# Attention with 64-wide heads: outputs moved ahead of undivided transposes, separate PSUM banks for scores, reciprocal sums through DRAM and scaled on GpSimd

## The chip, the core and the metric

The kernel runs on one core of a Trainium2 chip. The metric is the time of one launch in microseconds of the device. The engines are named as the profile names them: PE (TensorE), with its weight loads listed apart as PEld; DVE (VectorE), ACT (ScalarE), POOL (GpSimd), and SP (SyncE), which here only issues DMAs.

## What is computed

The program is four residual layers on x of shape 4 x 1024 x 256, float32: linear attention, a mixture of experts, causal softmax attention, and a second block with rotary attention and experts. The change touches the third layer alone. With a layernorm of x as its input (called x below) it computes

```python
q = (x @ Wq).reshape(B, S, 16, 64)
k = (x @ Wk).reshape(B, S, 16, 64)
v = (x @ Wv).reshape(B, S, 16, 64)
scores = einsum('bqhd,bkhd->bhqk', q / sqrt(64), k) + causal_mask
attn = softmax(scores, axis=-1)
out = einsum('bhqk,bkhd->bqhd', attn, v).reshape(B, S, 1024)
return x + out @ Wo
```

and the caller adds the layernorm of that to its residual. B is 4, S is 1024.

## The kernel before

The class `CausalAttention` (lines 670 to 923) works through 32 pairs: four batches, and in each eight pairs of heads, so that two heads of 64 fill the 128 rows of a tile. Each pair has eight steps, one for each block i of 128 query rows. The order of instructions on PE, DVE and ACT is written out by hand (`manual_schedule` in `run`, line 700); the order on POOL and SP is made by the scheduler.

For one step (b, hp, i) there are these parts:

- `scores` (L798): for one or two chunks of up to 512 keys, two matmuls, one for each head (L810), the heads in different halves of the array's rows. Blocks 0 to 3 have one chunk, blocks 4 to 7 have two. On DVE, a plain maximum over a full first chunk (L824), and for the last chunk a custom operation that adds the causal mask, negates, and takes the minimum (L819). With two chunks, L830 takes the smaller of both minima. Then ACT makes the exponentials with this bias and sums them as it goes (L839).
- At blocks 3 and 7 the end of `scores` turns the sums of four blocks into reciprocals on DVE (L850 to L853), and GpSimd spreads them over 64 columns for each head (L855).
- `turn` (L858): the exponentials are transposed in blocks of 128 (L867), four to a PSUM bank. The banks are copied to SBUF by `Ctx.copy`, which gives copies to DVE (L100) and ACT (L102) by turns. `turn` is called twice a step, with one half of the banks each; the second call also transposes the spread reciprocals at blocks 3 and 7 (L875) and copies them by ACT into rT (L879).
- `values` (L881): outputs as v times the transposed exponentials (L891), the two heads in different halves of the array's columns, into the bank ps_o, which holds four blocks. After blocks 3 and 7, DVE multiplies ps_o by rT into oT (L902).

Beside them, at blocks 2, 3 and 4, `project` makes q, k (L788) and v (L775) of the next pair, one for each block. In the first pair of batches 1 to 3, `finish` multiplies the previous batch's oT by Wo (L909), and `add` puts its layernorm onto x. The layernorms' powers run on POOL (L116), as do these additions (L921); the sums are stored by SP (kept, L923). In the last pairs of a batch, `measure`, `norm` and `flip` prepare the next batch's input.

The order within a step is that of the loop in `run`: scores of the next step, first half of `turn` for this step, the preparations and projections, `values` of the step before, second half of `turn`. On PE, ACT and DVE instructions start in that order.

PSUM has eight banks. Seven of them rotate under one tag, `bank`, for scores, transposes, projections and everything else of this stage (L805); the eighth is ps_o.

Of the kernel before, what the change touches and what calls it, by code (L numbers as in the profile page):

```python
# [9 lines left out]
F32 = mybir.dt.float32  # L10
# [3 lines left out]
ALU = mybir.AluOpType  # L14
# [5 lines left out]
P = 128  # L20
# [4 lines left out]
TPB = L // P  # L25
# [10 lines left out]
H3, HD3 = 16, 64  # L36
# [5 lines left out]
MASK = -(2.0**100)  # L42
# [627 lines left out]
class CausalAttention:  # L670
# [5 lines left out]

    NP = H3 // 2
    G = 4

    def __init__(self, k, pool, Wq, Wk, Wv, Wo):  # L680
        nc = k.nc
        self.k, self.pool = k, pool
        self.wq = per_chunk(nc, pool, Wq, "l1_wq")
        self.wk = per_chunk(nc, pool, Wk, "l1_wk")
        self.wv = per_chunk(nc, pool, Wv, "l1_wv")
        self.wo = pool.tile([P, self.NP, D], F32, name="l1_wo")
        nc.sync.dma_start(self.wo, Wo.rearrange("(c p) n -> p c n", p=P))

        self.wide_mask = pool.tile([P, 512], F32, name="l1_mask")
        nc.vector.memset(self.wide_mask, 0.0)  # L690
        nc.vector.tensor_copy(self.wide_mask[:, 512 - P :], k.mask)
        self.xn, self.xT, self.qk, self.v, self.oT = {}, {}, {}, {}, {}
        self.st, self.added = {}, {}
        self.e, self.eT, self.o, self.sums, self.r = {}, {}, {}, {}, {}

    def run(self, x, kept):

        pairs = [(b, hp) for b in range(B) for hp in range(self.NP)]
        steps = [(b, hp, i) for b, hp in pairs for i in range(TPB)]
        with self.k.tc.manual_schedule(engines=ENGINES):  # L700
            for j in range(TPB):
                self.measure(x, 0, j)
            for j in range(TPB):
                self.norm(x, 0, j)
                self.flip(0, j)
            for w in range(3):
                self.project(0, 0, w)
            self.scores(steps[0])
            for n, step in enumerate(steps):
                b, hp, i = step  # L710
                if n + 1 < len(steps):
                    self.scores(steps[n + 1])
                self.turn(step, 0)
                if b + 1 < B:

                    at = n % (self.NP * TPB) - (self.NP - 3) * TPB
                    if 0 <= at < TPB:
                        self.measure(x, b + 1, at)
                    if 0 <= at - 5 < TPB:
                        self.norm(x, b + 1, at - 5)  # L720
                    if 0 <= at - 7 < TPB:
                        self.flip(b + 1, at - 7)
                after = n // TPB + 1
                if 2 <= i < 5 and after < len(pairs):
                    self.project(*pairs[after], i - 2)
                if b > 0:

                    at = hp * TPB + i - 1
                    if 0 <= at < TPB:
                        self.finish(b - 1, at)  # L730
                    if 0 <= at - 2 < TPB:
                        self.add(x, b - 1, at - 2, kept)
                if n > 0:
                    self.values(steps[n - 1])
                self.turn(step, 1)
            self.values(steps[-1])
            for j in range(TPB + 2):
                if j < TPB:
                    self.finish(B - 1, j)
                if j >= 2:  # L740
                    self.add(x, B - 1, j - 2, kept)
# [56 lines left out]
    def scores(self, step):  # L798
        k, nc, pool = self.k, self.k.nc, self.pool
        b, hp, i = step  # L800
        qT, kT = self.qk[b, hp]
        n = (i + 1) * P
        parts, nms = [], []
        for c in range(0, n, 512):
            w = min(512, n - c)  # L805
            last = c + w == n
            ps = [k.bank("ps_s") for _ in range(2)]
            for a in range(2):
                rows = slice(a * HD3, (a + 1) * HD3)
                nc.tensor.matmul(  # L810
                    ps[a][:, :w], qT[rows, i * P : (i + 1) * P], kT[rows, c : c + w],
                    start=True, stop=True,
                )
            nm = k.small.tile([P, 2], F32, tag="nm3", name="nm", bufs=6)
            for a in range(2):
                s = ps[a][:, :w]
                if last:

                    nc.vector.tensor_tensor_reduce(  # L819
                        out=s, in0=s, in1=self.wide_mask[:, 512 - w :], scale=-1.0,  # L820
                        scalar=-MASK, op0=ALU.add, op1=ALU.min, accum_out=nm[:, a : a + 1],
                    )
                else:
                    nc.vector.tensor_reduce(nm[:, a : a + 1], s, AX.X, ALU.max, negate=True)  # L824
            parts.append((c, w, ps, -1.0 if last else 1.0))
            nms.append(nm)
        nm = nms[0]
        if len(nms) > 1:
            nm = k.small.tile([P, 2], F32, tag="nm3", name="nm", bufs=6)
            nc.vector.tensor_tensor(nm, nms[0], nms[1], ALU.min)  # L830
        if i % self.G == 0:
            self.sums[b, hp, i // self.G] = k.small.tile(
                [P, self.G, 2, i // self.G + 1], F32, tag=f"sums{i // self.G}", name="sums", bufs=2
            )
        sums = self.sums[b, hp, i // self.G]
        es = [pool.tile([P, L], F32, tag="e", name="e", bufs=4)[:, :n] for _ in range(2)]
        for c, w, ps, sign in parts:
            for a in range(2):
                nc.scalar.activation(  # L839
                    es[a][:, c : c + w], ps[a][:, :w], AF.Exp, bias=nm[:, a : a + 1], scale=sign,  # L840
                    accum_out=sums[:, i % self.G, a, c // 512 : c // 512 + 1],
                )
        self.e[step] = [e[:, t * P : (t + 1) * P] for e in es for t in range(i + 1)]
        self.eT[step] = []
        if i % self.G == self.G - 1:

            sums = self.sums.pop((b, hp, i // self.G))
            r = k.small.tile([P, self.G, 2], F32, tag="r3", name="r3", bufs=2)
            if i // self.G:
                nc.vector.tensor_tensor(r, sums[:, :, :, 0], sums[:, :, :, 1], ALU.add)  # L850
                nc.vector.reciprocal(r, r)  # L851
            else:
                nc.vector.reciprocal(r, sums[:, :, :, 0])  # L853
            wide = pool.tile([P, self.G, 2, HD3], F32, tag="rw", name="rw", bufs=1)
            nc.gpsimd.tensor_copy(wide, r.unsqueeze(3).to_broadcast([P, self.G, 2, HD3]))  # L855
            self.r[step] = wide

    def turn(self, step, half):  # L858

        k, nc, pool = self.k, self.k.nc, self.pool  # L860
        blocks = self.e[step]
        banks = [blocks[c : c + 4] for c in range(0, len(blocks), 4)]
        at = len(banks) // 2
        for some in banks[at:] if half else banks[:at]:
            pt = k.bank("ps_eT")
            for j, block in enumerate(some):
                nc.tensor.transpose(pt[:, j * P : (j + 1) * P], block, k.ident)  # L867
            eT = pool.tile([P, 512], F32, tag="eT", name="eT", bufs=8)
            k.copy(eT[:, : len(some) * P], pt[:, : len(some) * P])
            self.eT[step] += [eT[:, j * P : (j + 1) * P] for j in range(len(some))]  # L870
        if half == 1 and step in self.r:
            wide = self.r.pop(step)
            pt = k.bank("ps_r")
            for j in range(self.G):
                nc.tensor.transpose(  # L875
                    pt[:, j * P : (j + 1) * P], wide[:, j].rearrange("p a d -> p (a d)"), k.ident
                )
            self.rT = pool.tile([P, self.G * P], F32, tag="rT", name="rT", bufs=2)
            nc.scalar.copy(self.rT, pt)  # L879

    def values(self, step):  # L881
        k, nc, pool = self.k, self.k.nc, self.pool
        b, hp, i = step
# [4 lines left out]
        at = i % self.G * P  # L888
# [7 lines left out]
        if i % self.G == self.G - 1:  # L896
            part = b, i // self.G
            if hp == 0:
                self.oT[part] = pool.tile(
                    [P, self.NP, self.G * P], F32, tag="oT", name="oT", bufs=2  # L900
                )
            nc.vector.tensor_tensor(self.oT[part][:, hp, :], self.o, self.rT, ALU.mult)  # L902

    def finish(self, b, j):
        k, nc = self.k, self.k.nc
# [872 lines left out]
def sandwich(ctx, tc, w, out):  # L1778
# [23 lines left out]
                    moe.always(b - 1)  # L1802
        moe.run(x)
    with ExitStack() as stage:
        k.open_psum(stage, "psum3", banks=7)
        pool = stage.enter_context(tc.tile_pool(name="attn", bufs=1, reuse_waits="tile"))
        attn = CausalAttention(k, pool, w["Wq1"], w["Wk1"], w["Wv1"], w["Wo1"])
        attn.run(x, kept)
    with tc.tile_pool(name="keep", bufs=1, reuse_waits="tile") as keep:
        with ExitStack() as rope:  # L1810
# [76 lines left out]
```

## Time and profile before

| what | us |
|---|---|
| median of three runs (lowest to highest) | 3917.28 (3915.67 to 3919.04) |
| the profiled execution, its own time | 4002.54 |
| its span, first to last instruction | 4000.8 |
| this stage within the span | 967 to 2405 |
| ps_s L810, PE busy, 1536 records | 349.0 |
| ps_eT L867, PE busy, 2304 records | 351.0 |
| ps_o L891, PE busy, 4608 records | 317.7 |
| ps_r L875, PE busy, 256 records | 38.4 |
| e L839, ACT busy, with its sums | 437.0 |
| oT L902, DVE, 64 of | 0.692 each |
| rw L855, POOL, 64 of | 0.616 each |

A float32 matmul appears as two records, a transpose as one. A profile row gives the engine, the line of the kernel, and what is written and read ("ps_eT<-ident,e"), then, in the timeline, start and duration, and in brackets how long the engine had been idle and what ended that. The end of a matmul is modelled, so what PE really does is better read from the starts of its weight loads (PEld), each of which must wait for the bank or operand that its matmul needs.

### The profile page before, as it was taken

Reading aid. Unit: us, or ns where it says so; the run is one execution under the profiler, and the core shown is the slowest. Engines: PE = TensorE matmul, PEld = TensorE weight load, DVE = VectorE, ACT = ScalarE, POOL = GpSimd, SP = SyncE. Lnnn points to the kernel's source line nnn. Section 1 sums busy time; section 2 is a strip of 40 time slices with the busy share of each in tenths; the row PEclk is TensorE's granted clock in tenths of the full one; section 3 lists DMA queues with packets and bytes.
Section 4 is the critical chain, followed back from the end, with each engine's and each line's share of the span. In section 5 each row is a group of like instructions: output and inputs, shape, how many; then the busy total and the mean of one; then the engine's idle time right before and its main releaser. Section 6 shows DMA issues by size and latency. Waiting matters only on the chain.

```text
span 4000.8 us, 55924 instructions
## 1 busy us (share of the span) xinstructions
PE 3562.7 (89%) x21560; PEld 2224.5 (56%) x21560; DVE 1904.2 (48%) x5757; ACT 1480.0 (37%) x3593; POOL 786.2 (20%) x1088
## 2 busy tenths in 40 slices
PE   5899988867999999999999995999898997799982
PEld 4555666634666766766676673344334443466652
DVE  3645211145556556555655554667667574211124
ACT  1231111113555355445535542456455544011111
POOL 0101566552000100010010003222121111211033
PEclk7798999988999999999999997899899998799996
DMA  2001455521000000000000000000000001433213
GB/s 73 22 22 33 129 155 157 149 72 63 1 1 1 12 1 1 1 12 1 1 9 4 1 4 23 1 6 6 6 4 9 1 8 21 100 85 74 74 53 121
DMA packets 90882, 151.50 MB, mean 38 GB/s; under 512 B 19923, under 2 KB 66966, under 8 KB 90486
## 3 DMA queue, kind: packets, MB, share of 16 engines
q0 software_dynamic: 24816, 77.59, 7.5%
q1 hardware_dynamic: 42710, 47.51, 3.8%
q10 hardware_dynamic: 23088, 22.81, 1.7%
q8 instruction: 170, 2.79, 0.3%
q14 instruction: 98, 0.80, 0.1%
HBM read 112.35 MB, written 35.52 MB: 37 GB/s over the span
## 4 chain that ended last, share of the span: by engine, by line
PE 78%; DVE 9%; issue 4%; ACT 3%; POOL 2%; another core or an unknown queue 2%; DMA 1%; SPq 0%; ACTq 0%; POOLq 0%; DVEq 0%
PE ps_s L810 8%; PE ps_eT L867 7%; PE ps_gu L549 7%; PE ps_o L891 7%; PE ps_main L1253 7%; PE ps_qk L788 6%; PE ps_y L1751 6%; PE ps_h L1741 5%; PE ps_sums L1337 4%; PE ps_y L566 3%; PE ps_v L775 3%; PE ps_wo L909 3%; PE ps_exp L1309 2%; PE ps_main L1418 2%
## 5 line engine op out<-in xcount | busy, mean ns | idle before, releaser
L839 ACT ACTIVATE e<-ps_s,nm 128x512 f32<-128x512 f32 (+3 forms) x768 | 437.0, 578 | 491.1 <-DVE nm L830 332.0
L1316 ACT ACTIVATE et<-ps_exp 128x512 f32<-128x512 f32 (+3 forms) x744 | 325.5, 490 | 299.3 <-PE ps_exp L1309 263.6
L1309 PE MATMUL ps_exp<-qT,kT 32*128 32x512 f32 (+3 forms) x1488 | 408.4, 561 | 5.4 <-ACT et L1316 3.2
L1253 PE MATMUL ps_main<-kT,qT 32*128 32x512 f32 (+3 forms) x1488 | 384.0, 562 | 3.4 <-DVE nm L1266 2.5
L867 PE MATMUL ps_eT<-ident,e 128*128 128x128 f32 x2304 | 351.0, 284 | 6.2 <-ACT e L839 6.2
L810 PE MATMUL ps_s<-kT,qT 64*128 64x512 f32 (+3 forms) x1536 | 349.0, 521 | 1.6 <-ACT e L839 1.1
L891 PE MATMUL ps_o<-eT,v 128*64 128x128 f32 x4608 | 317.7, 279 | 3.3 <-DVE eT L100 3.2
L867 PEld LDWEIGHTS ps_eT<-ident,e 128*128 128x128 f32 x2304 | 243.4, 140 | 138.1 <-issue 62.3
L1266 DVE CUSTOM_DVE_ANT_0 ps_main<-ps_main,wide_mask 128x512 f32<-128x512 f32 (+1 forms) x488 | 230.8, 514 | 171.0 <-PE ps_exp L1309 122.3
L891 PEld LDWEIGHTS ps_o<-eT,v 128*64 128x64 f32 x4608 | 251.1, 136 | 102.0 <-issue 70.0
L819 DVE CUSTOM_DVE_ANT_0 ps_s<-ps_s,l_mask 128x128 f32<-128x128 f32 (+3 forms) x512 | 240.9, 512 | 54.4 <-PE ps_s L810 51.1
L549 PE MATMUL ps_gu<-moe_xTb,moe_w 128*128 128x256 f32 (+1 forms) x936 | 218.9, 384 | 46.9 <-DVE hT L557 31.8
L824 DVE TENSOR_REDUCE nm<-ps_s 128x1 f32<-128x512 f32 x256 | 166.7, 687 | 186.0 <-PE ps_s L810 186.0
L855 POOL COPY rw<-r 128x512 f32<-128x512 f32 x64 | 39.3, 615 | 1080.4 <-DVE r L851 651.9
L557 DVE TENSOR_TENSOR hT<-sg,ps_gu 128x256 f32<-128x256 f32 (+1 forms) x165 | 80.4, 495 | 343.4 <-ACT sg L556 145.8
L1741 PE MATMUL ps_h<-xT,w 128*128 128x512 f32 x512 | 227.4, 603 | 12.9 <-issue 12.9
L1253 PEld LDWEIGHTS ps_main<-kT,qT 32*128 32x128 f32 x1488 | 139.0, 195 | 179.5 <-issue 60.1
L102 ACT COPY eT<-ps_eT 128x512 f32<-128x512 f32 x320 | 169.0, 551 | 174.8 <-PE ps_eT L867 174.8
L1746 ACT ACTIVATE hTe<-ps_h,b 128x1024 f32<-128x1024 f32 x64 | 71.2, 1114 | 433.8 <-PE ps_h L1741 388.8
L1751 PE MATMUL ps_y<-w,hTe 128*128 128x256 f32 x1024 | 225.3, 382 | 4.2 <-ACT hTe L1746 4.2
L100 DVE COPY eT<-ps_eT 128x512 f32<-128x512 f32 (+1 forms) x320 | 197.3, 623 | 53.3 <-PE ps_eT L867 52.0
L1751 PEld LDWEIGHTS ps_y<-w,hTe 128*128 128x128 f32 x1024 | 196.1, 192 | 35.5 <-ACT hTe L1746 5.1
(366 smaller groups left out, 5858.7 us busy)
## 6 DMA issues: line engine op xcount, KB each, us to landing
w<-in_W SPq DMA_DIRECT2D x16, 1024.0 KB
moe_out<-moe_yb ACTq DMA_DIRECT2D x39, 256.0 KB
slots_out<-y ACTq DMA_DIRECT2D x8, 1024.0 KB
x<-in_x SPq DMA_DIRECT2D x4, 1024.0 KB
moe_in<-moe_xn ACTq DMA_DIRECT2D x4, 1024.0 KB
kept<-x SPq DMA_DIRECT2D x16, 256.0 KB
rows_in<-t SPq DMA_DIRECT2D x32, 128.0 KB
xo<-kept SPq DMA_DIRECT2D x8, 512.0 KB
```

The lines of the kernel that those rows point to most:

```text
L549: nc.tensor.matmul(ps[:n, half * 512 : half * 512 + W], w[:, c, f * P : f * P + n], xT[:, c, cols], start=(c == 0), stop=(c == NC - 1),)
L788: nc.tensor.matmul(ps, w[:, c, hp * P : (hp + 1) * P], xT[:, c, h : h + 512], start=(c == 0), stop=(c == NC - 1),)
L810: nc.tensor.matmul(ps[a][:, :w], qT[rows, i * P : (i + 1) * P], kT[rows, c : c + w], start=True, stop=True,)
L819: nc.vector.tensor_tensor_reduce(out=s, in0=s, in1=self.wide_mask[:, 512 - w :], scale=-1.0, scalar=-MASK, op0=ALU.add, op1=ALU.min, accum ...
L839: nc.scalar.activation(es[a][:, c : c + w], ps[a][:, :w], AF.Exp, bias=nm[:, a : a + 1], scale=sign, accum_out=sums[:, i % self.G, a, c // ...
L867: nc.tensor.transpose(pt[:, j * P : (j + 1) * P], block, k.ident)
L891: nc.tensor.matmul(self.o[a * HD3 : (a + 1) * HD3, at : at + P], v[:, t, a, :], eT[a * (i + 1) + t], start=(t == 0), stop=(t == i),)
L1253: self.k.nc.tensor.matmul(ps[:, :w], self.qT[b, h][rows, g, i % 4 * P : (i % 4 + 1) * P], self.kT[b, c // 512][rows, g, :w], start=True, s ...
L1309: self.k.nc.tensor.matmul(ps, self.kT[b, t // 4][rows, g, t % 4 * P : (t % 4 + 1) * P], self.qT[b, h][rows, g, off:], start=True, stop=True,)
L1316: self.k.nc.scalar.activation(et[:, r, 512 - ps.shape[1] :], ps, AF.Exp)
L1741: nc.tensor.matmul(ps[:, h : h + 512], w1[:, c, f * P : (f + 1) * P], xT[:, c, h : h + 512], start=(c == 0), stop=(c == NC - 1),)
L1751: nc.tensor.matmul(ps[:, :D], hT[:, f, s * P : (s + 1) * P], w2[:, f, :], start=(f == 0), stop=(f == nf - 1),)
```

## The change

Five things change together.

- The order of a step becomes: scores of the next step, `values` of the step before, then the whole of `turn` for this step, then preparations, projections and `finish` (which comes one step earlier than it did).
- Scores get four PSUM banks of their own (tag `s`). The other uses share the remaining three; ps_o keeps its bank.
- The plain maximum of the first chunk goes as a starting scalar into the custom operation of the last chunk, so that L830 is gone.
- The spreading on GpSimd and the transposes of reciprocals are gone. Instead SP stores the reciprocals to DRAM, transposed, in two DMAs, and reads them back in two, each broadcast over 64 partitions, into rT.
- ps_o is copied to oT by `Ctx.copy`, and GpSimd multiplies oT by rT in place.

```diff
-    def __init__(self, k, pool, Wq, Wk, Wv, Wo):
+    SB = 4
+    def __init__(self, k, pool, dram, Wq, Wk, Wv, Wo):
...
+        self.r_there = [
+            dram.tile([2, self.G, P], F32, name=f"l1_r{g}") for g in range(TPB // self.G)
+        ]
...
                 if n + 1 < len(steps):
                     self.scores(steps[n + 1])
-                self.turn(step, 0)
+                if n > 0:
+                    self.values(steps[n - 1])
+                self.turn(step)
...
-                    at = hp * TPB + i - 1
+                    at = hp * TPB + i
...
-                if n > 0:
-                    self.values(steps[n - 1])
-                self.turn(step, 1)
...
-            ps = [k.bank("ps_s") for _ in range(2)]
+            ps = [
+                k.psum.tile([P, 512], F32, tag="s", name="ps_s", bufs=self.SB) for _ in range(2)
+            ]
...
+                    least = nms[0][:, a : a + 1] if nms else -MASK
                     nc.vector.tensor_tensor_reduce(
                         out=s, in0=s, in1=self.wide_mask[:, 512 - w :], scale=-1.0,
-                        scalar=-MASK, op0=ALU.add, op1=ALU.min, accum_out=nm[:, a : a + 1],
+                        scalar=least, op0=ALU.add, op1=ALU.min, accum_out=nm[:, a : a + 1],
                     )
...
-        nm = nms[0]
-        if len(nms) > 1:
-            nm = k.small.tile([P, 2], F32, tag="nm3", name="nm", bufs=6)
-            nc.vector.tensor_tensor(nm, nms[0], nms[1], ALU.min)
+        nm = nms[-1]
...
-            wide = pool.tile([P, self.G, 2, HD3], F32, tag="rw", name="rw", bufs=1)
-            nc.gpsimd.tensor_copy(wide, r.unsqueeze(3).to_broadcast([P, self.G, 2, HD3]))
-            self.r[step] = wide
+            self.totals(step)
+
+    def totals(self, step):
...
+        there = self.r_there[g]
+            for a in range(2):
+                nc.sync.dma_start(there[a].rearrange("j q -> q j"), r[:, :, a])
+        rT = self.r[b, hp, g] = self.pool.tile([P, self.G * P], F32, tag="rT", name="rT", bufs=3)
+        for a in range(2):
+            nc.sync.dma_start(
+                rT[a * HD3 : (a + 1) * HD3],
+                there[a].rearrange("j q -> (j q)").partition_broadcast(HD3),
+            )
...
-        banks = [blocks[c : c + 4] for c in range(0, len(blocks), 4)]
-        at = len(banks) // 2
-        for some in banks[at:] if half else banks[:at]:
+        for c in range(0, len(blocks), 4):
+            some = blocks[c : c + 4]
...
-        if half == 1 and step in self.r:
-            wide = self.r.pop(step)
-            pt = k.bank("ps_r")
-            for j in range(self.G):
-                nc.tensor.transpose(
-                    pt[:, j * P : (j + 1) * P], wide[:, j].rearrange("p a d -> p (a d)"), k.ident
-                )
-            self.rT = pool.tile([P, self.G * P], F32, tag="rT", name="rT", bufs=2)
-            nc.scalar.copy(self.rT, pt)
...
-            nc.vector.tensor_tensor(self.oT[part][:, hp, :], self.o, self.rT, ALU.mult)
+            oT = self.oT[part][:, hp, :]
+            k.copy(oT, self.o)
+            nc.gpsimd.tensor_tensor(oT, oT, self.r.pop((b, hp, i // self.G)), ALU.mult)
...
-        k.open_psum(stage, "psum3", banks=7)
+        k.open_psum(stage, "psum3", banks=7 - CausalAttention.SB)
```

## The prediction

> **What bounds the kernel now.** I looked first at the stage that the change touches, 967 to 2405 us of the span, and at one head pair inside it, in the busy times by window (columns: window, length, then busy us and instructions of PE, PEld, DVE, ACT, POOL, then clock, DMA share, GB/s):
> ```profile
> 967.00:2405.00 1438.00, 1426.85 (x10752) 968.22 (x10752) 805.97 (x2242) 702.19 (x2027) 93.04 (x148) 1.00 0.01 4
> 1151.05:1192.61 41.56, 41.38 (x321) 27.39 (x321) 25.56 (x74) 21.82 (x64) 3.41 (x6) 1.00 0.01 1
> ```
> PE looks busy for 99% of it, at full clock, beside half-busy DVE and ACT. [...] PEld is 66%. By busy time, nothing but PE work counts, and the change would save the 38.4 us busy of the ps_r transposes: 3917 - 38 = 3879. By weight loads, PE has room for waits, and these decide. I go by the second.
>
> So I read PE from one weight load to the next. The timeline of a middle pair, first the step that starts with scores of block 5, then the one of block 7:
> ```profile
> 1151.05 0.30 PEld L810 LDWEIGHTS ps_s<-kT,qT 64*128 64x128 f32 x4 [0.17 <-issue]
> ...
> 1152.21 1.29 DVE L824 TENSOR_REDUCE nm<-ps_s 128x1 f32<-128x512 f32 x2 [2.19 <-PE ps_s L810]
> ...
> 1153.42 0.42 DVE L819 CUSTOM_DVE_ANT_0 ps_s<-ps_s,l_mask 128x256 f32<-128x256 f32 x1
> 1153.76 0.14 DVE L819 DVE_READ_ACCUMULATOR2_ANT nm<- 128x1 f32 x1
> ...
> 1154.31 0.16 DVE L830 TENSOR_TENSOR nm<-nm 128x2 f32<-128x2 f32 x1
> ...
> 1154.57 0.69 ACT L839 ACTIVATE e<-ps_s,nm 128x512 f32<-128x512 f32 x1 [2.77 <-DVE nm L830]
> ...
> 1156.36 0.48 ACT L839 ACTIVATE e<-ps_s,nm 128x256 f32<-128x256 f32 x1
> ...
> 1156.81 0.59 ACT L102 COPY v<-ps_v 128x512 f32<-128x512 f32 x1
> ```
> ```profile
> 1163.15 0.29 PEld L810 LDWEIGHTS ps_s<-kT,qT 64*128 64x128 f32 x2 [0.23 <-ACT e L839]
> ...
> 1164.94 0.29 PEld L810 LDWEIGHTS ps_s<-kT,qT 64*128 64x128 f32 x2 [0.27 <-ACT e L839]
> ...
> 1167.27 0.69 ACT L839 ACTIVATE e<-ps_s,nm 128x512 f32<-128x512 f32 x1 [1.42 <-DVE nm L830]
> ...
> 1169.94 0.87 ACT L102 COPY eT<-ps_eT 128x512 f32<-128x512 f32 x2
> ...
> 1170.16 0.17 DVE L850 TENSOR_TENSOR r<-sums 128x8 f32<-128x8 f32 x1 [2.99 <-ACT e L839]
> ```
> ACT takes nothing else until a step's exponentials are done: 5.8 us after S(5) began, 6.8 after S(7). After S(7) DVE waits for them too. Copies of transposes queue behind. PE survives this now because seven banks rotate. The waits by pair of waiter and releaser give the same picture (us in total, times, longest):
> ```profile
> ACT e L839 <- DVE nm L830: 332.0, 128, 3.6
> ...
> DVE r L850 <- ACT e L839: 94.6, 32, 3.0
> ...
> PEld ps_s L810 <- ACT e L839: 34.9, 123, 0.5
> ```
>
> **The yardstick.** S(i), O(i), T(i) are the scores, outputs and all transposes of block i; a prime marks the next pair. Scores' first weight loads stand at 1151.05, 1158.53, 1163.15, 1169.28, 1174.69, 1177.59, 1179.44, 1185.48 and 1192.61, so the steps that begin with S(5), S(6), S(7), S(0'), S(1'), S(2'), S(3'), S(4') take 7.48, 4.62, 6.13, 5.41, 2.90, 1.85, 6.04 and 7.13: 41.56 a pair.
>
> Slots on PE, also from the weight loads: a transpose 0.107; an output record 0.053; a 512-wide score pair 0.85, narrower in proportion; q or k 3.63; v 3.77; and 0.17 to 0.20 at each change between scores, outputs and full-tile work.
>
> **Part by part.** (1) *ps_r goes.* Four transposes are 0.43, twice a pair: -0.85. ACT loses its 0.59 copy, off the path. (2) *Outputs move ahead of undivided transposes.* Scores-half-outputs-half becomes scores-outputs-transposes: one tile change less in seven steps of eight, 7 x 0.17 = -1.19. (3) *The minimum (L830) goes.* Exponentials of head 0 can start after its own mask row: 1153.76 + 0.14 + 0.04 = 2.89 after S(5), not 3.52; S(7) likewise 3.18 instead of 4.12. Whether the mask operation takes longer with a scalar from memory no row shows: between 0 and about 0.4 us (both heads' rows then come before ACT starts); I take 0, as L121, which reads two such scalars for 256 elements, takes 0.41 like the plain 256 copy, 0.42.
>
> (4) *Three banks for everything but scores and ps_o.* I took the order of the built changed program, which names the instruction each one waits for, and laid the durations above along it, from each step's start:
>
> S(5): S 1.49, O(3) 1.02, T(4) from 2.51 to 3.58 in three banks. v needs T(4)'s first bank, which ACT copies after the exponentials: 2.89 + 0.67 + 0.67 + 0.45 + 0.45 = 5.13, copy to 5.72, 0.14 for the release: 5.86. A wait of **2.28**. v 3.77: step **9.63**.
> S(6): 1.71 + O(4) 1.24 + T(5) 1.45 = **4.40**, no wait.
> S(7): its second pair needs the bank of S(6)'s last exponential, free at 5.63 of the step before: **0.35**, O(5) at 2.25, T(6) at 3.71. T(6)'s fourth bank is its first, copied by ACT after 3.18 + 4 x 0.67 = 5.86, free at 6.59 where PE came at 4.99: **1.60**. Step **6.97**. DVE, held by the reciprocal to 6.4, copies the second bank by 7.08, soon enough.
> S(0'): 0.41 + O(6) 1.66 + T(7) 1.88 with **0.14** for the fourth bank: **4.09**.
> S(1'): **2.90** and S(2'): **1.85**, as before; ps_o is copied by ACT at 3.31, needed at 3.79.
> S(3'): O(1') needs T(1')'s copy, behind the exponentials of S(2'): **0.59**. With O(1'), T(2') and q: **6.51**.
> S(4'): 1.28 + 0.81 + 0.85 + k 3.63 = **6.57**.
>
> Sum 42.92, of which 4.96 is new waits. Without these PE needs 37.96; today's 41.56 is that plus 0.85, 1.19 and 1.55 of waits which go. So 3.60 gained, 4.96 lost: **+1.36 a pair**. Late next is ACT's copy queue, and behind it DVE's.
>
> (5) *Reciprocals through DRAM; GpSimd scales.* Per group SP issues two stores of 512 four-byte elements and two broadcasting loads. [...] The rows: the bias load (L1704), also four-byte elements, ran at 7 GB/s, so 2 KB takes 0.3 us; a kept store ended some 1.7 us after its issue. Two rounds of 1.7 and 0.3 with four issues of about 0.4 are an estimated 5 to 6 us. r is ready 6.3 us after S(7), its oT is copied at 6.97 + 4.09 + 3.31 = 14.4: 8 us of cover. GpSimd's product lies near twice L921's 0.725 us for 256 columns, 1.5 us, where the stage leaves POOL idle 94%; ps_o is freed by the copy, before it. The projection L909 reads oT in the next batch, four steps (over 15 us) after the last product of its part. Behind a late product on POOL stand only the rstd powers and adds L921, used two steps later; behind r's DMAs on SP stand kept stores, used a thousand us later. I take 0; without cover it would be at most 6 x 64 = 380 us, below zero nothing, since nobody waited for ps_o's old multiply beyond one step. The old 0.69 multiply becomes a copy of 0.69 or 0.59.
>
> (6) *Around the steady pairs.* 31 pairs with a successor: 31 x 1.36 = 42. In three pairs L909 stands in each step; its bank waits for DVE after T(6), 0.42, and before it hid some 1 us of waits that are gone, while it now hides 0.6 to 0.9: about +1 each, +3. Flips take banks at the same spots, +1; the last pair and tail +2. Together **+48**. The profiled execution, 4002.54 (span 4000.8), should become 4050. It is 85 us above the median, but this stage ran at clock 1.00 throughout, so the same 48 go on the median: 3917 + 48 = **3965**.
>
> **Rivals.**
> *Bank waits hurt (favoured), 3965, from 3935 to 3995*: an error of 0.9 a pair is 30 us. For it: both long waits follow from orders I can see. 0.62.
> *Exponentials start late, 4010*: the mask operation with a scalar from memory costs what L830 did, or ACT still starts after both heads. Then v waits 0.43 more, T(6) 0.65, O(1') some 0.3: 1.4 x 32 = +45. For it: no row shows such an operand. Against: single-chunk steps start after one head already (ACT at 1175.95, the second head's row at 1176.15). With a late rT here too. 0.18.
> *The banks come in time, faster, 3882*: one mechanism, the hold of ACT's copies behind exponentials. If it is shorter, or copies find ACT free, the waits fall; half of 4.96 leaves 3.60 - 2.48 = 1.1 x 32 = 35 us gained. It decides from the point where the waits sum to less than 3.60, that is, where the two long ones each shrink by 0.7. For it: half-busy ACT. Against: ACT is idle before, not after, the exponentials. 0.12.
> *Gains and waits cancel, 3917*: 0.08.
>
> **Numbers.** A measurement can tell 0.2%, 8 us. Slower: 0.62 + 0.18 = 0.80; same 0.08; faster 0.12. The range 3912 to 4025 leaves out the faster case and the far end of the late one. All weight is on the slower side.
>
> **What would show it.** Steps of about 9.6, 4.4, 7.0, 4.1, 2.9, 1.9, 6.5, 6.6 between scores' loads; a wait near 2.3 before ps_v and near 1.6 before the seventh block's last transposes, both released by ACT eT; no L830; exponentials 2.9 after S(5); POOL products without anyone waiting. Wrong if ps_v follows T(4) at once, if L909 waits for oT, or if PE loads show other slots.

## The result, and the profile after

| | before | after |
|---|---|---|
| median of four runs, us | 3918.16 | 4012.06 |
| lowest to highest | 3915.67 to 3919.22 | 4009.56 to 4013.11 |
| the profiled execution: its time, its span | 4002.54, 4000.8 | 4009.56, 4007.7 |
| from the scores of the first step to those of the last, us | 1397.2 | 1493.8 |

The change makes the kernel slower: 1.024 times the time before, 95% interval 1.0222 to 1.0257, so +94 us where +48 was forecast. The stage that the change touches is what moved. From the first weight load of its first step's scores to that of its last step's scores it became 96.6 us longer; from here on, "the stage" is this stretch. The two profiled executions differ by only 7 us because that of before was 85 us over its median: its stage begins at 966.8 us, and the other's at 891.8.

The busy times by window of the changed kernel (the columns are those of the first fence of the prediction; the third from the end is the granted clock): a stretch that holds the stage, one middle pair, and 3.4 us inside that pair.

```profile
892.00:2426.00 1534.00, 1398.67 (x10496) 972.21 (x10494) 778.38 (x2082) 684.77 (x1995) 133.29 (x148) 0.97 0.08 15
1414.65:1458.95 44.30, 40.56 (x314) 27.87 (x313) 22.16 (x57) 21.31 (x63) 2.52 (x2) 0.96 0.07 13
1439.40:1442.80 3.40, 3.40 (x18) 3.40 (x18) 0.69 (x1) 0.00 (x0) 0.00 (x0) 0.50 0.00 0
```

The pair takes 44.30 us, not the 42.92 that the prediction summed. And the clock is no longer 1.00: the last line lies wholly within one of 26 windows of 3.41 us in which the stage ran at half clock. Before, there was none.

The steps of that pair, in the prediction's order from S(5) to S(4'), beside the forecast. Of the 25 pairs that have no flip and no L909 in this step, 17 have 11.22 in S(5), or nearly so, and eight the value of the last line:

```
              S(5)   S(6)  S(7)  S(0')  S(1')  S(2')  S(3')  S(4')
forecast      9.63   4.40  6.97  4.09   2.90   1.85   6.51   6.57
measured     11.22   4.41  6.89  4.02   2.90   1.80   6.50   6.54
other pairs   9.59
```

Seven steps agree within 0.1 us, and so does the eighth, in the pairs where all of it runs at full clock. The timeline shows what happens in it, from the scores of block 5 to those of block 6:

```profile
1432.40 0.30 PEld L816 LDWEIGHTS ps_s<-kT,qT 64*128 64x128 f32 x4 [0.76 <-issue]
...
1434.91 1.07 PEld L884 LDWEIGHTS ps_eT<-ident,e 128*128 128x128 f32 x10 [0.17 <-issue]
...
1435.34 0.69 ACT L843 ACTIVATE e<-ps_s,nm 128x512 f32<-128x512 f32 x1 [4.00 <-DVE nm L826]
...
1437.13 0.48 ACT L843 ACTIVATE e<-ps_s,nm 128x256 f32<-128x256 f32 x1
...
1437.58 0.87 ACT L102 COPY eT<-ps_eT 128x512 f32<-128x512 f32 x2
1438.23 5.28 PEld L779 LDWEIGHTS ps_v<-l_wv,xT 128*128 128x128 f32 x32 [2.24 <-ACT eT L102]
...
1443.62 0.30 PEld L816 LDWEIGHTS ps_s<-kT,qT 64*128 64x128 f32 x4
```

PE finishes T(4), waits 2.24 us for ACT's copy of the first bank (forecast 2.28), and the copy stands behind the four exponentials, which began 2.94 us after S(5) (forecast 2.89). All that is as forecast. But then the weight loads of v last 5.28 us. In the kernel before they took 3.65, and v a slot of 3.77:

```profile
1152.93 3.65 PEld L775 LDWEIGHTS ps_v<-l_wv,xT 128*128 128x128 f32 x32
```

PE is let go at 1438.23, and at 1439.4 its clock is halved for 3.41 us.

The waits of that stretch, by waiter and releaser (us in total, times, longest):

```profile
POOL oT L912 <- DMA rT<-l_r: 787.0, 37, 31.2
...
PEld ps_v L779 <- ACT eT L102: 64.0, 28, 2.7
...
PEld ps_eT L884 <- ACT eT L102: 51.9, 32, 2.4
```

The two long waits are there. The first line is large and costs nothing by itself: POOL waits for rT, and no engine is listed as waiting for its products L912. But the transfers do cost something in another place. The DMA list (KB each, median us from issue to landing) has

```profile
rT<-l_r SPq DMA_DIRECT2D x128, 128.0 KB, 4.1
...
l_r<-r SPq DMA_DIRECT2D x128, 2.0 KB, 9.1
```

The list has a time for only two of the 128 stores, but SP's timeline shows all of them, because the loads are issued when the stores have landed: 7.9 to 10.5 us after the first store's issue, median 8.2. With the loads' 4.1 the round trip is some 12 us and not 5 to 6. In 10 of the 32 pairs steps S(2') and S(3'), which follow on the stores of blocks 4 to 7, become irregular. The clearest one in the timeline:

```profile
973.58 0.92 SPq L868 DMA_DIRECT2D l_r<-r  x2
...
978.15 0.69 DVE L100 COPY eT<-ps_eT 128x512 f32<-128x512 f32 x1 [0.21 <-PE ps_eT L884]
...
979.82 0.46 ACT L843 ACTIVATE e<-ps_s,nm 128x256 f32<-128x256 f32 x1
...
983.97 1.09 SPq L871 DMA_DIRECT2D rT<-l_r  x2
984.01 0.58 ACT L102 COPY oT<-ps_o 128x512 f32<-128x512 f32 x1 [3.64 <-remote]
984.12 0.43 DVE L100 COPY eT<-ps_eT 128x256 f32<-128x256 f32 x1 [4.48 <-remote]
...
984.67 0.23 PEld L899 LDWEIGHTS ps_o<-eT,v 128*64 128x64 f32 x4 [3.43 <-ACT oT L102]
```

ACT and DVE have nothing to wait for (PE's results for them were there at about 981), yet both stand still until 984.0, just when the stores of r have landed and SP issues the loads; PE then waits for ACT. In the stage 21 of the 121 packets that carry instructions take over 2 us, up to 3.9; before, none took over 1.5.

### The profile page after: what moved, and what is told of

Read it like the earlier page. It is cut to its first block, busy times and chain, and to the rows that moved or that the text cites. A ratio compares the mean times of both kernels' runs of the same rounds, so it can differ in the third digit from the quotient of the medians.

```text
span 4007.7 us, 55699 instructions
## 1 busy us (share of the span) xinstructions
PE 3513.9 (88%) x21304; PEld 2227.5 (56%) x21304; DVE 1877.3 (47%) x5597; ACT 1463.5 (37%) x3561; POOL 824.7 (21%) x1088
## 4 chain that ended last, share of the span: by engine, by line
PE 74%; DVE 10%; ACT 7%; issue 5%; POOL 3%; DMA 2%; SPq 0%; another core or an unknown queue 0%; DVEq 0%; POOLq 0%; ACTq 0%
PE ps_gu L549 8%; PE ps_main L1263 7%; PE ps_qk L792 6%; PE ps_s L816 6%; PE ps_y L1761 5%; PE ps_o L899 5%; PE ps_h L1751 5%; PE ps_eT L884 5%; ACT e L843 5%; PE ps_y L566 4%; PE ps_v L779 4%; PE ps_sums L1347 4%; PE ps_wo L919 3%; PE ps_exp L1319 2%; PE ps_main L1428 2%
## 5 line engine op out<-in xcount | busy, mean ns | idle before, releaser
L884 PE MATMUL ps_eT<-ident,e 128*128 128x128 f32 x2304 | 316.2, 280 | 45.9 <-ACT eT L102 44.3
L816 PE MATMUL ps_s<-kT,qT 64*128 64x512 f32 (+3 forms) x1536 | 330.1, 521 | 0.5 <-ACT e L843 0.5
L912 POOL TENSOR_TENSOR oT<-oT,rT 128x512 f32<-128x512 f32 x64 | 81.0, 1266 | 1160.5 <-DMA rT<-l_r 787.0
L816 PEld LDWEIGHTS ps_s<-kT,qT 64*128 64x128 f32 x1536 | 139.2, 186 | 139.0 <-issue 119.9
L779 PE MATMUL ps_v<-l_wv,xT 128*128 128x128 f32 x1024 | 155.8, 324 | 57.4 <-ACT eT L102 57.4
```

What stands on the lines that cost most here:

```text
L779: nc.tensor.matmul(ps[:, j * P : (j + 1) * P], xT[:, c, (h + j) * P : (h + j + 1) * P], self.wv[:, c, hp * P : (hp + 1) * P], start=(c == ...
L816: nc.tensor.matmul(ps[a][:, :w], qT[rows, i * P : (i + 1) * P], kT[rows, c : c + w], start=True, stop=True,)
```

## The experiments

The theory to be tested had three parts: too few banks outside of scores make PE wait for copies (B); each such wait brings a window at half clock (C); the packets of four bytes stall engines (D). The rivals: the new order costs the time, or the transfers and GpSimd's product do. Every kernel is compared with the kernel before on its own chip. In the first two groups of four that one took 3918.24 and 3917.74 us; in the last group 4006.19, with a later begin of the stage (961 to 973 us) as in the profile of before, so those four are read by their ratio and by their stage. The stage and the counts are those of the one profiled execution of each kernel.

| kernel | median us | ratio to before, 95% | stage us | half-clock windows | instruction packets over 2 us |
|---|---|---|---|---|---|
| before | | | 1397.2 | 0 | 0 |
| after | 4012.06 | 1.0222 to 1.0257 | 1493.8 | 26 | 21 |
| e1 seven shared banks | 3915.28 | 0.9982 to 0.9997 | 1397.3 | 7 | 20 |
| e2 copies on DVE | 3981.28 | 1.0146 to 1.0180 | 1461.8 | 20 | 25 |
| e3 wait filled | 4014.67 | 1.0235 to 1.0269 | 1497.4 | 15 | 25 |
| e4 no transfers | 3993.48 | 1.0183 to 1.0217 | 1475.5 | 22 | 0 |
| e5 seven banks, no transfers | 3887.85 | 0.9908 to 0.9942 | 1367.1 | 3 | 0 |
| e6 seven banks, rows by PE | 3909.16 | 0.9971 to 0.9985 | 1389.6 | 1 | 0 |
| e7 seven banks, sums on PE | 3923.43 | 1.0009 to 1.0022 | 1406.2 | 0 | 0 |
| e8 wait filled, no transfers | 3971.75 | 1.0121 to 1.0155 | 1453.1 | 4 | 0 |
| e9 old order, DRAM | 3977.69 | 0.9898 to 0.9938 | 1377.6 | 5 | 23 |
| e10 old order, rows by DVE | 3966.05 | 0.9883 to 0.9920 | 1362.1 | 0 | 0 |
| e11 new order, seven banks, rows by DVE | 3971.52 | 0.9897 to 0.9933 | 1369.9 | 0 | 0 |
| e12 old order, rows by DVE, chained minimum | 3939.48 | 0.9816 to 0.9850 | 1335.8 | 0 | 0 |

**e1: scores back in the shared seven banks.**

```diff
-            ps = [
-                k.psum.tile([P, 512], F32, tag="s", name="ps_s", bufs=self.SB) for _ in range(2)
-            ]
+            ps = [k.bank("ps_s") for _ in range(2)]
...
-        k.open_psum(stage, "psum3", banks=7 - CausalAttention.SB)
+        k.open_psum(stage, "psum3", banks=7)
```

> The changed kernel, but scores take their banks from one rotation of seven again, as they did before; order, sums by way of DRAM, GpSimd's product and the chained minimum stay. Theory (three banks for everything else make TensorE wait for copies, and the waits bring half-clock windows): both go, a steady pair falls from 44.3 us to the 38 us of its work plus up to 1, the pairs with wo lose their extra 6 us too; about 4012 - 32 x 5.8 = 3826 us (3795 to 3860), granted clock 1.00 all through the stage. Rival (the new order itself costs the time): the step that holds v and T(6) stays long, 3960 us or more. Rival (the DRAM path or GpSimd's product costs it): within 20 us of 4012.

Measured: 3915.28. The banks alone take back 97 us, which is the whole loss, so part B with C is right and both rivals are out as the main cause. But the 3826 was missed by 89. A steady pair takes 40.38 us, not 38 to 39: S(5) fell from 9.59 to 7.54 and S(7) from 6.89 to 5.22, while S(0') rose from 4.02 to 5.46. PE's weight loads show the wait that came up in this place:

```profile
PEld ps_o L897 <- ACT eT L102: 79.3, 82, 2.9
...
PEld ps_o L897 <- ACT oT L102: 25.9, 22, 4.3
```

Outputs now wait for copies of the transposes of the step before. And the irregular steps S(2') and S(3') are still there (pairs of 41 to 45 us).

**e2: the copies that PE waits for go to DVE.**

```diff
-            k.copy(eT[:, : len(some) * P], pt[:, : len(some) * P])
+            if step[2] in (4, 6):
+                k.turn ^= 1
+                nc.vector.tensor_copy(eT[:, : len(some) * P], pt[:, : len(some) * P])
+            else:
+                k.copy(eT[:, : len(some) * P], pt[:, : len(some) * P])
```

> The changed kernel with its four and three banks, but the copies of the transposes of blocks 4 and 6 all go to VectorE instead of taking turns, so that none of those that v and T(6) wait for stands behind exponentials on ScalarE. Theory: v's 2.3 us and most of T(6)'s 1.6 us go, and the half-clock windows behind them (1.6 us in a pair); a pair of about 39.5 us, about 3865 us (3835 to 3900). Rival (three banks are too few whoever copies): the wait moves on to the next bank and the time stays over 3960. Rival (DRAM path): within 20 us of 4012.

Measured: 3981.28, out of the theory's range and over 3960, as its first rival said. Step S(5) came down to 8.28, but S(7) rose from 6.89 to 7.41, since T(6) now waits for DVE instead of ACT:

```profile
PEld ps_eT L884 <- DVE eT L888: 68.5, 32, 3.0
```

DVE is behind the masks and reductions there as ACT is behind exponentials. Of the 20 windows at half clock that remain, 19 follow this wait, which lasted 1.94 to 2.98 us before them. Another engine for the copy cures one of the two waits; three banks stay too few for the other.

**e3: PE works through its wait for v.**

```diff
-                nc.tensor.transpose(pt[:, j * P : (j + 1) * P], block, k.ident)
+                for _ in range(self.FILL if step[2] == 4 and c == 8 else 1):
+                    nc.tensor.transpose(pt[:, j * P : (j + 1) * P], block, k.ident)
```

FILL is 9.

> The changed kernel, but TensorE does each of the two transposes in the third bank of T(4) nine times over (16 more in a pair, 1.7 us of its work at the rate of the others), so that it works through most of the 2.24 us in which it waits for v's bank. Clock theory: the wait as such keeps its end, but v no longer runs at half clock behind it; the step from S(5) to S(6) falls from 11.2 to 9.6 us in most pairs, about 4012 - 28 x 1.5 = 3970 us (3955 to 3985) with more work done. Rival (half-clock windows are not due to this wait, or stay for T(6)'s): 4005 to 4020. Rival (the transposes aren't hidden): 4012 + 32 x 1.7 = 4066.

Measured: 4014.67, the rival's number, and yet S(5) is 9.60 us in every steady pair: summed over the pairs that have a successor, this step fell from 337.7 to 310.8 us. The 27 us were given back in the same execution, by S(2') and S(3'), whose sum rose from 293.4 to 317.3, and by S(0'), 139.8 to 144.5. The run can't decide about the clock, since the stalls moved too. So these had to go first.

**e4: no transfers.**

```diff
-            nc.gpsimd.tensor_tensor(oT, oT, self.r.pop((b, hp, i // self.G)), ALU.mult)
+            nc.gpsimd.tensor_tensor(oT, oT, self.ones, ALU.mult)
```

with stores and loads of r taken out.

> The changed kernel without the four transfers per group: GpSimd multiplies by a tile of ones, so the sums are computed but not applied; all other work stays. Theory: the transfers cost only the few stalls in which ScalarE and VectorE waited for instructions behind the 4-byte packets: 10 to 25 us, so 3987 to 4002 us; pairs of 44.3 us and half-clock windows stay. Rival (transfers or their packets carry most of the loss): 3950 or less. Rival (they cost nothing): 4005 to 4020.

Measured: 3993.48, 18.6 us under the changed kernel. S(2') is 1.80 and S(3') 6.50 in every pair without further work, and no instruction packet takes over 1.5 us. That is in the forecast range: part D holds, with 18 us of the 94.

**e8: as e4, with the wait filled** (the edit of e3 on e4).

> Four and three banks, no transfers (sums not applied), and the 16 extra transposes in v's wait. Clock theory, with the irregular stalls out of the way: against the run without transfers alone (3993 us; 16 of its pairs have a step of 11.22 us) every such step falls to 9.60 us; 16 x 1.6 saved, 1.7 in each wo pair saved, some 7 us added where T(4) was not waited for: about 3968 us (3958 to 3980). Rival (half-clock windows come anyway and take the gain elsewhere): 3988 to 4000.

Measured: 3971.75. With nothing else moving, extra work on PE makes the stage 22.4 us shorter, and the windows at half clock fall from 22 to 4. In e4, 19 of them follow the wait for v's bank and three the wait of T(6); in e8 none follows v's and four follow T(6)'s. The same place in e8 (S(5) began at 1415.96; the first line is the last of the extra transposes):

```profile
1419.96 1.34 PEld L875 LDWEIGHTS ps_eT<-ident,e 128*128 128x128 f32 x12
...
1421.14 0.87 ACT L102 COPY eT<-ps_eT 128x512 f32<-128x512 f32 x2
...
1421.80 3.65 PEld L779 LDWEIGHTS ps_v<-l_wv,xT 128*128 128x128 f32 x32 [0.50 <-ACT eT L102]
...
1425.56 0.30 PEld L816 LDWEIGHTS ps_s<-kT,qT 64*128 64x128 f32 x4
```

v begins 5.84 us after S(5), as in the changed kernel (5.83), since ACT's copy is no earlier. But PE idled 0.50 us instead of 2.24, and the loads of v take 3.65 us instead of 5.28. The clock in e4 and in e8, over stretches that hold the stage:

```profile
887.00:2403.00 1516.00, 1391.64 (x10497) 967.66 (x10496) 779.40 (x2082) 685.61 (x1995) 134.09 (x148) 0.98 0.01 4
```
```profile
890.00:2383.00 1493.00, 1416.53 (x11006) 993.24 (x11005) 782.05 (x2082) 685.49 (x1995) 134.64 (x148) 1.00 0.01 4
```

Part C is shown for the wait of v. In the pairs with a flip and in the last one, where v had not waited, the extra transposes cost 3 x 1.8 + 1.75 = 7.1 us; so 18 windows fewer saved 22.4 + 7.1 = 29.5, or 1.64 each.

**e5: seven shared banks and no transfers** (e1 and e4 together).

> Seven shared banks as in the run before, and also no transfers: GpSimd multiplies by ones, so the sums are computed but not applied. Theory (4-byte packets hold up the loads of instructions, and engines starve in the steps of blocks 1 and 2): the irregular steps fall to 1.80 and 6.52 us in every pair and none of the instruction packets takes over 2 us; the excess of these steps with seven banks, added up over the pairs, is some 36 us, so 3915 - 36 = 3879 us (3870 to 3890). Rival (those steps are long for another reason that seven banks bring): 3905 or more.

Measured: 3887.85, in the forecast range, 27.4 under e1, and S(2') and S(3') are regular: what stalls cost depends on where they fall, 18 us with four and three banks, 27 with seven.

**e6: r is turned on PE and stored in rows.**

```diff
-        with nc.allow_non_contiguous_dma(reason="a transpose of 8 columns"):
-            for a in range(2):
-                nc.sync.dma_start(there[a].rearrange("j q -> q j"), r[:, :, a])
...
+        nc.tensor.transpose(pt[: 2 * self.G, :P], r.rearrange("p a j -> p (a j)"), k.ident)
...
+        nc.scalar.copy(r8, pt[: 2 * self.G, :P])
+        nc.sync.dma_start(there.rearrange("a j q -> (a j) q"), r8)
```

> Seven shared banks, and r goes to DRAM in rows of 512 bytes: TensorE turns r (128 x 8) into 8 x 128 after the transposes of blocks 3 and 7, ScalarE copies it, one store of 8 rows takes the place of two stores of 512 packets of 4 bytes; loads and product stay. Theory (it is the many 4-byte packets, not the way by DRAM): stalls vanish as without transfers, 64 transposes add about 0.15 us each, 3879 + 10 = 3889 us (3875 to 3900), which beats the kernel before. Rival (the loads of rT or the wait for DRAM bring the stalls): 3915 or more.

Measured: 3909.16, out of the theory's range. The stalls are gone though r still goes by DRAM, so it is the packets of four bytes that hurt; with rows, SP issues the loads 1.3 us after the store (median) instead of 8.2. But the pair takes 41.22 us, 0.84 more than in e5, and not 0.3; most of it is in the step of S(4'), 7.33 against 6.55. e7 has the same 7.33 there. Both use one bank and one ACT copy more after T(3) than e5; which of the two it is, no run shows.

**e7: the sums turned on PE as before, the rest as e1** (the code of before for rw, ps_r, rT and the product on DVE).

> Seven shared banks, new order and chained minimum, but the sums are turned on TensorE and multiplied on VectorE as before. Theory: no packets, so no irregular steps; 8 transposes in a pair add their 1.2 us: 3879 + 32 x 1.2 = 3917 us (3905 to 3930), about the kernel before: order and minimum are worth little together. Rival (the order is worth the 1.2 us of tile switches by itself): 3880 to 3900. Rival (the order costs): 3935 or more.

Measured: 3923.43, close to the forecast and a little slower than the kernel before (1.0009 to 1.0022). New order and chained minimum together bring nothing.

**e9: the old order with r by DRAM in packets of four bytes and GpSimd's product.** The kernel before, with this half of the change alone.

> The kernel before (old order, seven shared banks, old minimum) with the second half of the change alone: r by way of DRAM in packets of 4 bytes, GpSimd's product. Theory: the transposes of ps_r and their bank go, worth what they are worth in the new order (3923 - 3888 = 35 us, 1.55 us in a pair), and the irregular steps come back at some 27 us: 3918 - 35 + 27 = 3910 us (3895 to 3930); some twenty instruction packets over 2 us. Rival (in the old order PE waits at that place anyway, so only the stalls come): 3940 to 3950. Rival (stalls need the new order): 3883.

Measured: 28.5 us under the kernel before (0.9918), a larger gain than the 8 us expected, and than the range's 23. Stalls are back, with 23 long instruction packets, but S(2') and S(3') sum to 287.9 us against 266.3 in e10: 22 us where 27 were assumed. The stage of the profiled execution, which was the slowest of the four, gained only 19.6.

**e10: the old order, r turned by DVE and stored in rows of 128 bytes.** On e9:

```diff
-                for a in range(2):
-                    nc.sync.dma_start(there[a].rearrange("j q -> q j"), r[:, :, a])
+            rows = self.r_rows[g]
+            nc.vector.transpose(rows, self.r_wide[g])
+            for q in range(0, P, 32):
+                nc.sync.dma_start(
+                    there.rearrange("a j q -> (a j) q")[:, q : q + 32],
+                    rows[q : q + 2 * self.G],
+                )
```

> As the run before, but VectorE transposes r (padded to 128 x 32) in blocks of 32 x 32, and four stores of 8 rows of 128 bytes take the place of the 1024 packets of 4 bytes. Theory: no instruction packet over 2 us, no irregular step; 3918 - 35 = 3883 us (3870 to 3900). Rival (PE waits there anyway): 3910 to 3920. Rival (any store through DRAM brings the stalls): as the run before.

Measured: 40.1 us under the kernel before (0.9901), in the forecast range, and no stall; in the stage 35.1, where 35 was forecast. Reciprocals off PE, with what takes their place, are worth 1.2 us in a steady pair (41.56 to 40.34).

**e11: the changed kernel with seven shared banks and these rows.**

> The changed kernel with seven shared banks, and r turned by VectorE in blocks of 32 x 32 and stored in rows of 128 bytes. Theory: as without transfers (3888 us), 64 small VectorE operations more that nobody waits for: 3889 us (3880 to 3900). If the old order is as good as the new one, the run before gives the same within 10 us; rival (the new order, together with sums that need no TensorE, is better): over 10 us under it.

Measured: 34.7 us under the kernel before (0.9915), in the forecast range; a pair of 40.66 us. Beside e10 it looks as if the order made no difference. But e11 also has the chained minimum.

**e12: e10 with the chained minimum.**

```diff
-                        scalar=-MASK, op0=ALU.add, op1=ALU.min, accum_out=nm[:, a : a + 1],
+                        scalar=nms[0][:, a : a + 1] if nms else -MASK, op0=ALU.add, op1=ALU.min,
+                        accum_out=nm[:, a : a + 1],
...
-            nm = k.small.tile([P, 2], F32, tag="nm3", name="nm", bufs=6)
-            nc.vector.tensor_tensor(nm, nms[0], nms[1], ALU.min)
+        nm = nms[-1]
```

> The run with the old order and rows of 128 bytes, and the chained minimum too: 4 small VectorE operations less in a pair, 0.06 us more in each of the masking operations. If VectorE's time before the exponentials decides the steps, up to 4 x 0.06 us in a pair is gained or lost; expected within 10 us of the run without it, 3880 us (3865 to 3895). Rival (the chain makes the last masking wait for the first reduction): 3900 or more.

Measured: 66.7 us under the kernel before, 0.9833 (0.9816 to 0.9850): the fastest here, and 26.6 under e10 where at most 10 were expected. The expectation had counted DVE's time only. What counts is that the exponentials of head 0 need not wait for both masks and a minimum behind them (in S(5) they start at 2.94 us instead of 3.52); S(7) and S(0') shrink by 0.42 each. With the minimum equal, e12 and e11 differ in the order alone, and the new order is 34 us slower. PE's waits in the stage, first in e12, then in e11:

```profile
PEld ps_eT L884 <- ACT e L844: 32.3, 58, 2.0
PEld ps_eT L884 <- ACT eT L102: 25.3, 36, 0.8
...
PEld ps_o L899 <- ACT eT L102: 9.3, 28, 0.6
```
```profile
PEld ps_o L905 <- ACT eT L102: 72.0, 84, 1.7
...
PEld ps_o L905 <- DVE eT L100: 19.3, 33, 1.0
...
PEld ps_eT L890 <- ACT e L845: 2.2, 2, 2.0
```

In the old order half of a `turn` and the projections stand between scores and outputs, and the copies of the step before are done by then. In the new order outputs come right after scores and wait for them, 91 us against 9. Not all of that is lost, because in the old order transposes stand at this place and wait as well, 58 us against 2. The balance falls in two steps. S(0') takes 5.73 us in e11 and 4.81 in e12: O(6) waits 0.85 and 0.60 us where T(7) waited 0.38. S(3') takes 6.52 and 6.04: O(1') waits 1.39 us where T(2') waited 0.76. All other steps are equal within 0.16 us.

## Why the prediction was right in kind and short in size

Going from the kernel before to the changed one, one edit at a time, the stage takes:

| edit added | stage us | difference |
|---|---|---|
| kernel before | 1397.2 | |
| reciprocals off PE, rows by DVE, product on GpSimd (e10) | 1362.1 | -35.1 |
| chained minimum (e12) | 1335.8 | -26.3 |
| new order (e11) | 1369.9 | +34.1 |
| packets of four bytes for the rows (e1) | 1397.3 | +27.4 |
| four banks for scores, three for the rest (after) | 1493.8 | +96.5 |

(The rows come from different chips; at full clock their steps agree to 0.01 us, as 2.90 and 1.80 for S(1') and S(2') in all that have no stall and no reciprocals on PE.) Two parts that gain and two that cost some 30 us each cancel, and the split of the banks is the loss. Order and minimum give about the same sum elsewhere: +9.0 in e7, where the table has 34.1 - 26.3 = +7.8. But the sizes depend on the other parts present; the packets, for one, cost 18 us with split banks. Against the steps of the prediction:

- **The bank waits, part (4): right.** Which instruction waits for which copy, how long (2.24 for 2.28), the exponentials' start, and the eight steps, each within 0.1 us at full clock. Take e4, which has no stalls, and leave out its 22 half-clock windows at 1.64 us: 1475.5 - 36 - 1397.2 = +42, for the forecast +48. (That this leaves 42 rests on the estimate of 1.64 us for a window, from e8 and e4.)
- **The step that failed is the sum's clock:** "this stage ran at clock 1.00 throughout, so the same 48 go on the median". It ran so while PE's waits were short (in the middle pair at most 0.8 us, in the whole stage 2.0). The sum kept v's slot at 3.77 us behind a wait of 2.28; measured from v's first load to the next scores it is 5.39, and the step 11.22 instead of 9.63. Of the 28 waits for v's bank in the changed kernel (2.23 to 2.70 us), 20 came with 3.41 us at half clock; the step then took 11.22 us where it took 9.59 without (the pairs that have neither a flip nor L909), so that the wait cost itself and 1.6 us more. 22 windows are 36 us in e4, the largest term that the sum left out. In the changed kernel itself the windows are 26: 20 follow the wait of v, five that of T(6), one a stall.
- **Part (5) failed in size: "I take 0".** Its cover argument held: nobody waits for a late product, although GpSimd's product began 13.7 us after the first store's issue (median) and not 5 to 6. But it asked only who waits for r, and not what is held up while 1024 packets of r go through: +18 us, including the 4 windows that e4 hasn't. 42 + 36 + 18 is the growth of the stage; the three add up by construction, so what tests the forecast is the 42 beside its 48.
- **Part (1)** put the reciprocals' transposes at 0.85 us a pair; taking them off PE was worth 1.2; what goes beyond their slots is not traced. **Part (3)** was right: exponentials start 0.6 us earlier, the first head's mask operation takes 0.06 us more with a scalar from memory (0.48 against 0.42 for 128 x 256, medians), the second head's 0.02.
- **Part (2) was wrong as a reason.** The tile changes saved are real (S(4') and S(6) are about 0.15 us shorter in e11 than in e12), but the order also moves outputs ahead of their operands. The forecast "without these PE needs 37.96" left out these waits: with seven banks a pair takes 40.66. In the sum it did no harm, since the waits for banks hid the waits for operands.
- **The rivals.** "Exponentials start late", 4010, has the measured time and is wrong: they start at 2.94 us. The forecast range had been stretched to 4025 for this rival, so it is luck that 4012 lies in it. "The banks come in time", 3882, has a kernel now: e5, 3887.85, where the banks do; it also has no transfers, and its outputs are not scaled.

What stays open is how four-byte packets stop ACT and DVE. That instructions are loaded late behind them fits that both stop at once with their inputs there, that they go on about when the stores land, and that instruction packets of 8 and 16 KB take over 2 us, up to 3.9, only in kernels with these stores (20 to 25 such packets in each). But the long packets don't lie at each stall (none at 980 to 984), so this is inferred and not shown. Nor is it shown what of the stores is still under way then: their four-byte packets are recorded at 974.5 to 975.4, and they land at 984.

## What to carry to other kernels

A wait on PE can cost more than its own length: from the trace of before, list the waits that a change adds to PE, and where one is as long as those that half clock followed here (2.1 to 2.7 us in the changed kernel, 1.94 to 2.98 in e2, though not each time), allow for some 1.6 us more behind it. When a pool of banks is split, follow the release of each bank in program order, and ask on which engine's queue the release stands and behind what; when an operation is moved ahead, ask the same of its operands. And a transfer that nobody waits for need not be free: here the transfers of r, with 1024 packets of four bytes for each group, cost 18.6 us in the changed kernel and 27.4 with seven banks. Turn the data first, and send rows; with rows no stall was left in e6 and e10.

## What the runs showed of the hardware that was not expected

The half-clock windows of the changed kernel's stage are all recorded as 3.413 us long, and they begin multiples of 3.413 us apart, 11 of the 25 times 44.37 us (13 times 3.413). A steady pair takes 44.29 us, only 0.08 less, so that the same place is hit pair after pair.

What PE did ahead of them can be counted. Divide the stage into stretches of 3.413 us in step with these windows, and add up the gaps of over 0.25 us between weight loads in each. All 26 windows at half clock followed a stretch of which PE had idled 0.58 to 0.78, and no other stretch had more than 0.63; so from 0.58 to 0.63 both outcomes occur in this trace. In e2 and e6 some windows followed on 0.49 to 0.57 by the same count. No run shows a limit. In the eight pairs with 9.59 in S(5) the wait was as long as elsewhere (2.23 to 2.24 us), but it lay across a boundary of these stretches, with at most 0.56 of a stretch on either side, and no window at half clock followed there.

With the 16 extra transposes in PE's wait in e8, none of the 19 windows that followed v's wait in e4 was left, and the clock over the stage was 1.00 instead of 0.98. And a transpose of 128 x 32 by DVE with four stores of 8 rows of 128 bytes did the same as 1024 packets of four bytes, without a stall, and SP issued the loads 2.2 us after the first store (median, in e10) instead of 8.2.
